# Two channels in a 32-row tile: a product-quantized convolution pair regrouped from 88 tiles of three channels to 128 tiles of two

## The chip, the cores and the metric

The kernel runs on one core of one Trainium2 chip. The metric is the device time of one execution in microseconds (us), the median of several executions. A ratio is the mean time of one kernel's runs over the mean time of the other kernel's runs of the same rounds, with a 95% interval; it is therefore not quite the ratio of the medians that stand beside it.

Names: TensorE is PE in the profile, VectorE is DVE, ScalarE is ACT, GpSimd is POOL, SyncE is SP.

Words: an engine *issues* a transfer, and the transfer *lands* when the last of its end records comes in. A *turn* is a transpose on VectorE. *Half clock* is a stretch in which the trace records a granted TensorE clock of 0.5, and one such stretch is a *spell*. The *maxima* are the largest logits of a softmax, taken out before the exponential.

## The reference

Sixteen images of 256 channels and 28x28 pixels go through group norm, then twice through a convolution in which every 3x3 patch of every channel is replaced by a softmax mixture of that channel's 16 centroids. Batch norm, a squeeze-and-excite gate and two residual additions follow.

```python
def amm_conv3x3(x, centroids, w_sub, stride=1):
    B = x.shape[0]
    C, k, s = centroids.shape                       # 256, 16, 9
    patches = jax.lax.conv_general_dilated_patches(x, (3, 3), (stride, stride), 'SAME')
    p = patches.reshape(B, C, s, Ho * Wo).transpose(0, 3, 1, 2)
    d = jnp.sum(p * p, axis=-1)[..., None] - 2.0 * jnp.einsum('bncs,cks->bnck', p, centroids) \
        + jnp.sum(centroids * centroids, axis=-1)[None, None]
    attn = jax.nn.softmax(-d, axis=-1)
    lut = jnp.einsum('cks,cso->cko', centroids, w_sub)
    return jnp.einsum('bnck,cko->bno', attn, lut)...
# per image: x + relu(se(bn2(amm(relu(bn1(amm(gn(x))))))) + gn(x))     [cut]
```

## The kernel before

An image's two layers are worked in halves of 384 and 400 pixels. The nine shifted copies of the image (the patches) are written to DRAM by ScalarE (`to_pat`) and loaded again as rows of tiles (`patches`). A tile of 32 rows holds three channels. The 88 tiles make 11 groups of eight, so two halves and two layers make 44 slots per image. A slot has one group of *logits* (eight products of 31x64), the exponential of it, one group of *numerators* (eight products of 64x32) of the slot before, and three or four *lookups* (full 128x128 products that add the result into two accumulators).

```python
def to_pat(l, i, pat):                               # patch writes, ScalarE's hardware queue
    dx, pieces = STEPS[i]
    for j, k, p0, n, rt in (PIECES[i] for i in pieces):
        ...
        nc.scalar.dma_start(view(pat, ...), ...)

def finish(b, k, i):                                 # last residual of an image, four times per image
    y, xt = ys[b][0][half(k, i)], xs[b][half(k, i)]
    rstd, _ = nrm[b]
    nc.vector.scalar_tensor_tensor(y, xt, rstd[:, k : k + 1], y, op0=ALU.mult, op1=ALU.add)
    nc.vector.scalar_tensor_tensor(y, y, 0.0, xt, op0=ALU.max, op1=ALU.add)

def patches(u):                                      # one load of 128 rows for two groups, GpSimd's software queue
    ...
    nc.gpsimd.dma_start(
        pt[:, : 2 * len(gs), :n],
        view(u["pat"], 2 * gs[0] * P * HW + px, [[HW, P], [P * HW, 2 * len(gs)], [1, n]]),
    )

def logits(u, gi, rows):
    l, g, n = u["l"], u["groups"][gi], u["px"][1]
    ps = [pair(), pair()]
    for i in range(4):
        for h in range(2):
            nc.tensor.matmul(
                ps[i // 2][64 * h : 64 * h + 64, i % 2, :n],
                lhsT=wd[l][32 * i : 32 * i + rows, 2 * g + h, :],
                rhs=u["pt"][32 * i : 32 * i + rows, 2 * gi + h, :n],
                start=True, stop=True,
            )
    return ps

# the order inside the program, slot s of a group (the second number is the place in the slot)   [cut]
at(s, 5, b_logits, u, gi)
at(s, 6, b_exp, u, gi)
at(s + 1, 3, b_num, u, gi)                           # numerators one slot after their exp
at(s + 1, 4, b_turn, u, gi)
at(s + 1, 4, c_scale, u, gi)
at(s + 2, 2, c_turn, u, gi)
at(n - self.lead - (self.lb if mx else 0), 9, patches, u)
```

Some tiles of the second layer also need their maxima first. Their logits are computed once ahead, reduced on VectorE, sent to DRAM and back on SyncE (`m_out`, `m_in`) into the tile `pm`.

## Time and profile before

| | before |
|---|---|
| median of 3 runs | 3248.12 us (3246.1 to 3253.05) |
| span of the profiled run | 3240.9 us, clock 0.980 |
| TensorE / VectorE / ScalarE / GpSimd busy | 95% / 76% / 46% / 41% |
| image period in the quiet part | 188.6 us |

TensorE is the bound; the lines that carry this are shown in the prediction below.

### The profile page before, as it was taken

Reading aid. Unit: us, or ns where it says so; the run is one execution under the profiler, and the core shown is the slowest. Engines: PE = TensorE matmul, PEld = TensorE weight load, DVE = VectorE, ACT = ScalarE, POOL = GpSimd, SP = SyncE. Lnnn points to the kernel's source line nnn. Section 1 sums busy time; section 2 is a strip of 40 time slices with the busy share of each in tenths; the row PEclk is TensorE's granted clock in tenths of the full one; section 3 lists DMA queues with packets and bytes.
Section 4 is the critical chain, followed back from the end, with each engine's and each line's share of the span. In section 5 each row is a group of like instructions: output and inputs, shape, how many; then the busy total and the mean of one; then the engine's idle time right before and its main releaser. Section 6 shows DMA issues by size and latency. Waiting matters only on the chain.

```text
span 3240.9 us, 72313 instructions
## 1 busy us (share of the span) xinstructions
PE 3079.0 (95%) x29086; PEld 1208.6 (37%) x29086; DVE 2479.0 (76%) x4133; ACT 1506.0 (46%) x2507; POOL 1330.1 (41%) x1427
## 2 busy tenths in 40 slices
PE   3489999999999999999999999999999999999997
PEld 2233333333333333333333333333333333334333
DVE  2156778788787878878787887878788787878786
ACT  1144455454545545454544545445454545545343
POOL 1033444444444444444443444444344444434342
PEclk7689999999999999999999999999999999999999
DMA  7465555575655557565555756555575555556532
GB/s 228 119 191 170 166 177 178 175 230 178 195 184 176 179 173 230 178 195 183 176 175 177 229 179 194 176 175 181 180 229 179 194 180 177 178 177 220 173 111 65
DMA packets 232373, 586.02 MB, mean 181 GB/s; under 512 B 76238, under 2 KB 89182, under 8 KB 232030
## 3 DMA queue, kind: packets, MB, share of 16 engines
q0 software_dynamic: 76544, 321.16, 31.9%
q10 hardware_dynamic: 82666, 238.70, 22.5%
q1 hardware_dynamic: 72820, 21.45, 3.3%
q8 instruction: 232, 3.80, 0.5%
q14 instruction: 111, 0.91, 0.1%
HBM read 328.23 MB, written 257.82 MB: 181 GB/s over the span
## 4 chain that ended last, share of the span: by engine, by line
PE 70%; DVE 17%; DMA 6%; POOL 3%; issue 2%; ACT 1%; SPq 0%; ACTq 0%; POOLq 0%; DVEq 0%
PE acc L722 38%; PE pair L571 17%; PE pair L645 13%; DVE nt L657 4%; DVE q L711 4%; POOL nt L684 3%; DVE rc L661 3%; DVE y L538 2%; DMA xt<-in_x 1%; DVE z L590 1%; DMA pat<-in_consts 1%; DVE gn_st L426 1%; DVE y L539 1%; DMA ws<-dws 1%; DMA dm<-mt 1%
## 5 line engine op out<-in xcount | busy, mean ns | idle before, releaser
L722 PE MATMUL acc<-q,ws 128*128 128x384 f32 (+1 forms) x4608 | 1732.9, 511 | 0.6 <-ACT y L745 0.6
L635 ACT ACTIVATE e<-pair 128x768 f32<-128x768 f32 (+1 forms) x1408 | 1084.6, 821 | 1351.2 <-PE pair L571 1268.0
L684 POOL TENSOR_TENSOR nt<-nt,rc 128x648 f32<-128x648 f32 (+1 forms) x576 | 773.2, 1342 | 1404.6 <-DVE rc L661 1180.3
L722 PEld LDWEIGHTS acc<-q,ws 128*128 128x128 f32 x4608 | 811.3, 190 | 911.0 <-issue 463.6
L711 DVE STREAM_TRANSPOSE q<-nt 128x768 f32<-128x768 f32 (+1 forms) x576 | 577.6, 1003 | 424.7 <-POOL nt L684 380.0
L657 DVE STREAM_TRANSPOSE nt<-pair 128x768 f32<-128x768 f32 (+1 forms) x704 | 692.3, 983 | 157.2 <-PE pair L645 153.9
L645 PE MATMUL pair<-e,cw 64*32 64x384 f32 (+1 forms) x11264 | 639.2, 505 | 60.6 <-ACT e L635 49.3
L571 PE MATMUL pair<-pt,wd 31*64 31x384 f32 (+1 forms) x9216 | 558.1, 517 | 9.1 <-DVE z L590 9.1
L661 DVE RECIPROCAL rc<-nt 128x72 f32<-128x72 f32 (+1 forms) x704 | 438.6, 623 | 24.2
L690 POOL TENSOR_TENSOR qx<-nt,rc 128x324 f32<-128x324 f32 (+3 forms) x256 | 179.0, 739 | 406.8 <-DVE rc L661 406.8
L645 PEld LDWEIGHTS pair<-e,cw 64*32 64x32 f32 x11264 | 131.0, 105 | 440.4 <-ACT e L635 207.0
L700 ACT COPY nt<-qx 128x120 f32<-128x120 f32 (+1 forms) x576 | 184.5, 320 | 238.0 <-DVE rc L661 228.7
L571 PEld LDWEIGHTS pair<-pt,wd 31*64 31x64 f32 x9216 | 143.3, 130 | 400.0 <-issue 340.2
L556 POOL DMA_DIRECT2D pt<-pat x288 | 228.6, 794 | 36.2 <-DMA pat<-side 35.9
L590 DVE STREAM_TRANSPOSE z<-pair 128x768 f32<-128x768 f32 (+1 forms) x192 | 182.7, 989 | 68.9 <-PE pair L571 68.9
L571 PE MATMUL pair<-pm,wd 31*64 31x384 f32 (+1 forms) x3584 | 224.9, 513 | 6.9 <-DVE nt L657 5.4
L596 DVE TENSOR_REDUCE mx<-z 128x48 f32<-128x768 f32 (+1 forms) x192 | 186.2, 970 | 0.0
L664 DVE TENSOR_REDUCE ext<-rc 128x1 f32<-128x72 f32 (+1 forms) x608 | 140.5, 231 | 20.8
L665 DVE TENSOR_REDUCE ext<-rc 128x1 f32<-128x72 f32 (+1 forms) x608 | 134.2, 221 | 0.0
L571 PEld LDWEIGHTS pair<-pm,wd 31*64 31x64 f32 x3584 | 61.0, 129 | 146.5 <-issue 52.8
L556 POOL DMA_DIRECT2D pm<-pat x128 | 94.9, 742 | 8.6 <-DMA pat<-side 8.6
L538 DVE SCALAR_TENSOR_TENSOR y<-xt,gn_rstd,y 128x392 f32<-128x392 f32 x64 | 76.9, 1202 | 0.8 <-ACT y L532 0.8
(106 smaller groups left out, 720.6 us busy)
## 6 DMA issues: line engine op xcount, KB each, us to landing
pt<-pat POOLq DMA_DIRECT2D x144, 800.0 KB, 7.5
pt<-pat POOLq DMA_DIRECT2D x144, 768.0 KB, 5.7
pat<-side ACTq DMA_DIRECT2D x128, 771.8 KB
pat<-im ACTq DMA_DIRECT2D x64, 771.8 KB
pat<-side ACTq DMA_DIRECT2D x64, 404.2 KB
pm<-pat POOLq DMA_DIRECT2D x64, 400.0 KB, 6.1
xt<-in_x POOLq DMA_DIRECT2D x32, 784.0 KB, 8.0
pm<-pat POOLq DMA_DIRECT2D x64, 384.0 KB, 4.1
```

Of the source, the lines that this page charges most:

```text
L556: nc.gpsimd.dma_start(pt[:, : 2 * len(gs), :n], view(u["pat"], 2 * gs[0] * P * HW + px, [[HW, P], [P * HW, 2 * len(gs)], [1, n]]),)
L571: nc.tensor.matmul(ps[i // 2][64 * h : 64 * h + 64, i % 2, :n], lhsT=wd[l][32 * i : 32 * i + rows, 2 * g + h, :], rhs=u["pt"][32 * i : 32 ...
L590: nc.vector.transpose(z[:, : 64 * nb].rearrange("p (i m) -> p i m", i=2), ps[:, :, : 32 * nb])
L596: nc.vector.tensor_reduce(u["mx"][:, a : a + 2].rearrange("p i (c b) -> p i b c", c=2)[:, :, :nb], u["z", gi].pop(0)[:, : 64 * nb].rearran ...
L635: nc.scalar.activation(e[:, :, :n], ps[:, :, :n], AF.Exp, scale=2.0)
L645: nc.tensor.matmul(ps[32 * i : 32 * i + 32, h, :n], lhsT=cw[l][64 * h : 64 * h + 64, g, i, :], rhs=es[i // 2][64 * h : 64 * h + 64, i % 2, ...
L657: nc.vector.transpose(t[:, : 2 * nb].rearrange("p (h b) r -> p h (b r)", h=2), u.pop(("nm", gi))[:, :, : 32 * nb])
L661: nc.vector.reciprocal(rc[:, : 2 * nb], t[:, : 2 * nb, SUM : SUM + 3])
L684: nc.gpsimd.tensor_tensor(v, v, rc[:, : 2 * nb].unsqueeze(3).to_broadcast([P, 2 * nb, 3, 9]), ALU.mult)
L700: nc.scalar.copy(u["nt", gi][0][:, : 2 * nb].rearrange("p (h b) r -> p h b r", h=2)[:, :, :, SUM:], bass.AP(w.tensor, w.offset, [list(w.ap ...
L711: nc.vector.transpose(q[:, : 64 * nb], t[:, : 2 * nb].rearrange("p b r -> p (b r)"))
L722: nc.tensor.matmul(accs[key][:, :n], lhsT=ws[l][:, 2 * g + h, o * P : (o + 1) * P], rhs=u["q", gi][:, 32 * nb * h : 32 * nb * h + n], star ...
```

## The change

Its intent is less work on TensorE: a tile of 32 rows holds two channels, so a group is 16 products of 32x32 that run side by side instead of eight larger ones. Eight groups of sixteen tiles make 32 slots per image instead of 44, at nearly the same cost per group. The rest follows from that layout: patch tensors of 18 dense rows (no constant fill), four loads of 18 rows per tile on SyncE, dense numerators, numerators in the slot of their exp with lookups split around them, the second step of the finish on ScalarE and GpSimd, and the watch on the sums on GpSimd. The sorting of weights moves from the start into the first slots. (Where loads are counted, "tile" means the patches of one such group: one load tile that holds sixteen of the 32-row tiles.)

```diff
-NCH = 3
-NRT = 88
+NCH = 2
+NRT = 128
+ROWS = 9 * NCH
...
-    d_pat = [dram.tile([NRT * 32, HW], F32, name=f"pat{i}") for i in range(3)]
+    d_pat = [dram.tile([NRT * ROWS, HW], F32, name=f"pat{i}") for i in range(3)]
...
-    def clear_pat(i): ...            # constants into the patch tensors
+    for t in pts + pms:              # constants once, into fixed tiles (4 pts, 2 pms)
+        nc.sync.dma_start(t[ONE::32], ...)
...
     def to_pat(l, i, pat):           # 12 writes per image and layer, still on ScalarE
-        for j, k, p0, n, rt in (PIECES[i] for i in pieces):
-            nc.scalar.dma_start(...)
+        nc.scalar.dma_start(
+            view(pat, (ROWS * p0 + 9 * k + 3 * dx) * HW, [[ROWS * HW, n], [HW, 3], [1, HW]]), ...)
...
     def finish(b, k, i):
         nc.vector.scalar_tensor_tensor(y, xt, rstd[:, k : k + 1], y, op0=ALU.mult, op1=ALU.add)
-        nc.vector.scalar_tensor_tensor(y, y, 0.0, xt, op0=ALU.max, op1=ALU.add)
+        nc.scalar.activation(y, y, AF.Relu)
+        nc.gpsimd.tensor_add(y, y, xt)
...
     def patches(u):
-        nc.gpsimd.dma_start(pt[:, : 2 * len(gs), :n], ...)
+        for i in range(4):
+            nc.sync.dma_start(
+                pt[32 * i : 32 * i + ROWS, :, :n],
+                view(u["pat"], (16 * u["m"] + i) * ROWS * HW + px, [[HW, ROWS], [4 * ROWS * HW, 4], [1, n]]),
+            )
...
-    def logits(u, gi, rows):
-        for i in range(4):
-            for h in range(2):       # 8 products
+    def logits(u, rows):
+        for t in range(4):
+            for i in range(4):       # 16 products
+                c = 32 * ctile(i, t)
                 nc.tensor.matmul(
-                    ps[i // 2][64 * h : 64 * h + 64, i % 2, :n], ...
+                    ps[t // 2][c : c + 32, t % 2, :n], ...
...
+    LOGITS, EXP, LOOK_A, NUM, TURN, SMALL, LOOK_B, MAX, LOOK_C, TURN_BACK, REST = range(11)
```

## The prediction

No term of its sum is among them: it still comes to 174.9 + 8.4 + 2.9 + 1.5 + 3.5 + 1 = 192 us per image, of which the author took 190.

> **What bounds the kernel now.** I read the page first (busy shares and slices), then the chain of work that ended last, then a table over one stretch of it, then the timeline of a few microseconds inside it.
>
> ```profile
> PE 3079.0 (95%) x29086; PEld 1208.6 (37%) x29086; DVE 2479.0 (76%) x4133; ACT 1506.0 (46%) x2507; POOL 1330.1 (41%) x1427
> ...
> PE   3489999999999999999999999999999999999997
> ```
>
> TensorE (PE) is busy 95%; only the first three slices (81 us each) are thin. The chain of waits shows the steady rhythm, because the same burst of four lookup products comes back once per image:
>
> ```profile
> 2256.30 2.88 PE acc L722 x8
> 2322.09 2.88 PE acc L722 x8
> 2334.47 2.88 PE acc L722 x8
> 2350.67 2.88 PE acc L722 x8
> 2444.94 2.88 PE acc L722 x8
> ```
>
> 2444.94 - 2256.30 = 188.6 us per image. The table over that stretch (busy us of PE, weight loads, DVE, ACT, POOL, then clock, DMA share, GB/s):
>
> ```profile
> 2256.30:2445.00 188.70, 187.61 (x1809) 72.88 (x1810) 154.16 (x255) 93.28 (x155) 82.55 (x88) 1.00 0.60 188
> ```
>
> PE 99.4%, clock 1.00: here PE sets the time. 16 x 188.6 = 3018 us; the other 3241 - 3018 = 223 us is the start (the first logits group runs at 116 us and slots limp until 170) and some 20 us of end. The timeline shows one slot (columns: start, duration, engine, line):
>
> ```profile
> 1603.26 0.88 PE L645 MATMUL pair<-e,cw 64*32 64x384 f32 x16
> ...
> 1604.07 0.90 PE L571 MATMUL pair<-pt,wd 31*64 31x384 f32 x16
> 1604.42 0.94 DVE L657 STREAM_TRANSPOSE nt<-pair 128x768 f32<-128x768 f32 x1
> ...
> 1604.90 2.28 PE L722 MATMUL acc<-q,ws 128*128 128x400 f32 x6
> 1605.07 1.51 ACT L635 ACTIVATE e<-pair 128x768 f32<-128x768 f32 x2 [2.14 <-PE pair L571]
> 1605.40 0.60 DVE L661 RECIPROCAL rc<-nt 128x72 f32<-128x72 f32 x1
> ...
> 1607.11 0.88 PE L645 MATMUL pair<-e,cw 64*32 64x384 f32 x16
> ```
>
> To see: numerators (8 small products, 16 instructions[...]) hold PE from 1603.26 to 1604.07, 0.81 us; logits 0.83; three lookups 2.21. For the 400-column half the same starts give 0.84, 0.85; lookup bursts give 2.13 (3) and 2.78 (4) at 384 columns, 2.21 and 2.88 at 400, so about 0.19 per burst plus 0.66 per product. Exp starts 1.00 after the logits, two take 1.51, and they hide behind three or four lookups: numerators of a group run one slot later.
>
> Check of this arithmetic on before: per image 44 slots x (0.82+0.84) = 73.0; 144 lookups x 0.66 = 95.0; 50 bursts x 0.19 = 9.5; 6 extra logits groups 5.0; six waits of 0.47 after them (groups of 1.31 instead of 0.83) 2.8; small products about 2. Sum 187.3, measured 188.6.
>
> [...] Here first rounds of the 8 tiles start 6.7 ns apart in the trace[...]. [...] the new layout has four row tiles writing one bank, in different quadrants. No run shows that case yet; it is a risk. [...]
>
> **The change part by part, per image.**
>
> Small products. Groups fall from 44 to 32 for logits and for numerators, extra logits from 6 to 4. A group has 16 products, so eight more starts: 0.05 us (8 x 6.7 ns), giving 0.86 + 0.88 (384) or 0.89 + 0.90 (400), mean 1.77 for the pair. 32 x 1.77 = 56.6 against 73.0: saves 16.4.
>
> Lookups. 16 tiles of dense numerators and 2 of tails: 36 products per half image and layer, as before. 95.0 us stays. But they now stand in two bursts per slot (two between logits and numerators, two or three behind): 64 + 4 bursts x 0.19 = 13.0 against 9.5: loses 3.5. Extra logits 3.5 against 5.0; small products 2.
>
> Exp in the same slot. Two lookups after the logits end at 0.88 + 1.48 = 2.36 us after their start; the second exp is done at 1.00 + 1.51 + 0.06 (release to start as seen at 218.98) = 2.57. The second half of the numerators waits about 0.15: x 32 = 4.8.
>
> Sum so far 56.6 + 95.0 + 13.0 + 3.5 + 2 + 4.8 = 174.9, a slot of 5.27 us. This is 13.7 us (7%) less than before. DVE per slot: two transposes 0.97, reciprocal of 96 to 104 (604 ns for 72, 642 for 78, so 0.75 to 0.8), transpose back 1.0: 3.65 of 5.27. POOL: scaling 768 to 832 elements (1293 ns for 648) 1.6, tails and two sums 1.1: 2.7, which has a slot to hide in. ACT exp 1.54. None becomes the bound on average. The two range reductions (141 + 134 us), the fills (185 us ACT) and the POOL load issues (324 us) go from engines with room: worth nothing directly.
>
> **What is given back: work that crosses engines at the slot's end.**
> - The finish. The second DVE step becomes an ACT Relu and a POOL add. DVE reaches the first step only after turns, reciprocal and transpose back, 3.65 us after the numerators end; each takes 1.2. The two Relus (0.7) thus end at 5.6 and 6.75, two gates follow (1.4), and only then ACT takes the next exp, due at 2.8. PE waits for it: about 5.2 us, then 3.2 in the next slot, which has no gates. 8.4 per image. Before had both steps on DVE.
> - Group norm. Statistics fall in slots with the maximum work: DVE ends 6.9 us after the numerators where PE wants them after 5.3: 1.7. Two later hops through POOL cost about 0.5 and 0.7. Together 2.9.
> - Maxima. Between the turn of the maxima and the logits that use them are now some 7.5 us (17 before). The round trip through DRAM took 4.5 us when quiet and 8 to 15 beside patch writes. About 1.5.
> - DMA. Second-layer patches (7.2 MB) are written two pieces per slot, 228 GB/s, beside loads of 0.45 MB per slot[...]. At the start before's writes alone got about 240 GB/s, and issues blocked ACT up to 2.4 us. Estimate 3 to 4.
>
> 174.9 + 8.4 + 2.9 + 1.5 + 3.5 + 1 for evacuations = 192; with halves of these gains and losses in doubt I take 190.
>
> Start. No constant fill of the patch tensors (ACT sat 20.6 us behind it, later 18.3 again), and weight sorting (46 to 116 us) moves among the slots. First slot near 56, about 45 us of sorting products remain, plus 30 to 35 of stalls: 136 lost instead of 203. With 20 of end, 156 against 223: saves 67.
>
> **Sum:** 16 x 190 = 3040, less 8 for the last image's finish, plus 156 = 3188. I put 3190.
>
> **Rivals.**
> 1. The packing gain comes through whole: the ACT block is shorter than worked out. For it: 7% is a large and well-measured term. Against: [...]the program order is plain. Then 16 x 179 + 156 = 3020 to 3050.
> 2. Tiles sharing a bank, or 64 instructions per group, slow the groups by 0.1 us or more. For: [...]no group here has more than 32 instructions with weight loads. Against: [...]starts are 6.7 ns apart. 68 groups x 0.1 x 16 = 109 us: about 3300[...].
> 3. Transfers become the wait[...]. For: DMA already shows shares near 0.8 in bursts. Against: bytes fall (18 rows of 32 used), and loads are issued some four slots ahead. If exp and loads wait through both layers' writes, 5 to 10 us per image more: 3270 to 3350.
> 4. DVE becomes the bound. Its 3.65 of 5.27 us speaks against it, except in slots with maxima.
>
> **Range and chances.** The image period may be off by 7 us either way (112 us in all) and the start by 25: 3060 to 3320. The 2% line is 3183, almost at my value; rival 1 pulls below it, 2 and 3 above. Faster 0.45, same 0.45, slower 0.10.
>
> **What would show it.** Right: groups of 32 PE instructions lasting 0.86 to 0.90 from start to next burst; slots near 5.3; numerators waiting for ACT e in every slot by 0.1 to 0.2 and, twice per image, by 3 to 5 us with a Relu just ahead of that exp; a first slot near 56 us. Wrong: groups above 1.0 us; no long waits for exp; POOL or SyncE loads named ahead of logits; a period under 180 or above 200.

## More of the kernel before

One more view matters later, so it is given here: the waits of TensorE before (engine, line, what it waited for; then us in total, times, longest), from 270 to 3150 us of the span.

```profile
PE pair L571 <- DVE z L590: 9.1, 13, 1.8
PE pair L645 <- ACT e L635: 7.3, 4, 3.9
```

These are the two largest; all that the view lists come to 28 us in 2880, and none is a DMA. There is nothing to win from waits; only less work on TensorE can help.

## The result

| | before | after |
|---|---|---|
| median | 3249.12 us (3246.1 to 3253.05, 4 runs) | 3380.34 us (3372.49 to 3393.12, 4 runs) |
| ratio after/before | | 1.0407 [1.0371, 1.0443] |
| clock of the profiled run | 0.980 | 0.950 |

The change made the kernel slower by 4%, outside the predicted range. The outputs are correct. From the page after, busy times, the granted clock in 40 slices, and the chain that ended last by engine:

```profile
PE 3042.2 (90%) x39838; PEld 1195.0 (35%) x39838; DVE 2250.0 (67%) x2756; ACT 1094.9 (32%) x1611; POOL 1501.8 (45%) x2165
...
PEclk9888999999999999999999999999999999999998
...
PE 62%; DMA 16%; DVE 12%; issue 4%; ACT 2%; POOL 2%; SPq 1%; ACTq 1%; DVEq 0%; POOLq 0%
```

TensorE is no longer busy throughout (90% for 95%), and DMA now has 16% of the chain (6% before). The same table over one image period as in the prediction (busy us of PE, weight loads, DVE, ACT, POOL, then clock, DMA share, GB/s):

```profile
2057.01:2261.20 204.19, 186.76 (x2482) 72.54 (x2481) 139.35 (x168) 67.51 (x99) 93.42 (x134) 0.95 0.61 159
```

This period has 17 us in which TensorE is idle and a clock of 0.95. Measured from the first small product of the squeeze-and-excite step of one image to that of another, eleven images apart, the period is 200.6 us on average (190.2 before, measured in the same way). Predicted were 190.

The timeline of a few microseconds shows what is right and what is wrong (start, duration, engine, line, operation, tiles, shape, count; in brackets the idle time just before and its releaser):

```profile
2047.57 0.93 PE L543 MATMUL pair<-pt,wd 19*32 19x384 f32 x32
...
2049.96 1.09 PE L611 MATMUL pair<-e,cw 32*32 32x384 f32 x32
2050.98 1.61 PE L675 MATMUL acc<-q,ws 128*128 128x400 f32 x4
...
2053.19 0.83 PE L543 MATMUL pair<-pt,wd 19*32 19x384 f32 x4
2054.98 2.03 PE L543 MATMUL pair<-pt,wd 19*32 19x384 f32 x28 [0.96 <-DMA pt<-pat]
2056.95 2.93 PE L675 MATMUL acc<-q,ws 128*128 128x384 f32 x4
```

The logits group at 2047.57 takes 0.86 us to the next start, as worked out. The one at 2053.19 stops after four of its 32 instructions, because the other loads of its tile have not landed: the next two lookups (four instructions) start at 2056.95 instead of some 2054.05. And those lookups then take 2.93 us instead of 1.56 (the two at 2050.98 took 1.61 with 400 columns). The granted clock in the records is 0.5 from 2056.4 on, for 3.4 us. So this late load is paid twice: by the wait, and by TensorE at half clock after it.

The waits of TensorE after, from 270 to 3150 us:

```profile
PE pair L611 <- ACT e L601: 72.5, 42, 3.6
PE pair L543 <- DMA pm<-dm: 67.2, 23, 4.5
PE pair L543 <- DMA pt<-pat: 49.7, 24, 3.9
PE pair L409 <- DVE gn_mv L404: 23.5, 14, 1.7
```

In 28 us of waits before there was no DMA; now there are 117 us for transfers: patches (`pt<-pat`) and maxima (`pm<-dm`). The view even counts too little: a group that stops in its middle, as above, is shown with less idle time than it lost (0.96 us for the 1.8 us from 2053.2 to 2054.98), because the model of overlapping products covers part of the gap. I added up the gaps between the starts of neighbouring products in the trace, where the instruction between them waits for a semaphore of a SyncE or ScalarE transfer: 58.2 us within the logits groups (34 times). Most of these stops are in the view's 49.7 us already: 43.5 of them lie within groups and only 6.3 before a group. So the loads cost 6.3 + 58.2 = 64.5 us of waiting.

Why do loads come late? The queue of SyncE itself says what each load stood waiting for before it was issued (same window):

```profile
SPq L530 <- DMA pat<-im: 352.0, 68, 12.3
SPq L530 <- DMA pt<-pat: 348.1, 469, 4.7
SPq L582 <- DVE mt L575: 322.0, 48, 17.6
SPq L530 <- PE pair L543: 302.9, 197, 8.4
SPq L530 <- DMA pat<-side: 249.9, 84, 6.9
```

`pat<-im` and `pat<-side` are the patch writes of ScalarE. In none of these waits does the load read what the write is writing: that is a later stage's tensor. The instruction list explains it. Every transfer counts its end on a semaphore, and this program has eight for all transfers of SyncE and ScalarE together (numbers 108 and 110 to 116 in the trace) and eight others for GpSimd's (100 to 107). They are used strictly in turn: the 2407 issues of SyncE and the 392 of ScalarE, each in its own order, merge into one rotation over the eight, 349 or 350 times round. And none of the 2799 was issued before the last landing record that the trace holds of the previous user of its semaphore. Before, SyncE issued about 490 transfers, ScalarE 512 and GpSimd 464 (416 of them patch loads). After, SyncE issues 2407 and ScalarE 392 over the same eight, and GpSimd only 48. So a load waits for whatever stood eight transfers before it, and often that is a 588 KB write that ScalarE issued late. In all 152 of the waits for `pat<-im` and `pat<-side` above, the semaphore waited for is the one that the load itself is about to use. The maxima's transfers on SyncE stand behind writes in the same way, for 78 us in this window. The chain around the timeline above shows one such case (start, duration, what):

```profile
2039.68 7.37 DMA pat<-im
...
2047.07 0.02 SPq L530
...
2047.48 8.35 DMA pt<-pat
...
2055.87 1.15 PE pair L543 x26
2057.01 2.86 PE acc L675 x4
```

A write issued at 2039.68 lands at 2047.05; only then does SyncE issue the load (L530), which lands at 2055.83, and TensorE goes on.

### The profile page after: what moved, and what is told of

Read it like the earlier page. It is cut to its first block, busy times and chain, and to the rows that moved or that the text cites. A ratio compares the mean times of both kernels' runs of the same rounds, so it can differ in the third digit from the quotient of the medians.

```text
span 3371.0 us, 94072 instructions
## 1 busy us (share of the span) xinstructions
PE 3042.2 (90%) x39838; PEld 1195.0 (35%) x39838; DVE 2250.0 (67%) x2756; ACT 1094.9 (32%) x1611; POOL 1501.8 (45%) x2165
## 4 chain that ended last, share of the span: by engine, by line
PE 62%; DMA 16%; DVE 12%; issue 4%; ACT 2%; POOL 2%; SPq 1%; ACTq 1%; DVEq 0%; POOLq 0%
PE acc L675 35%; PE pair L611 13%; PE pair L543 12%; DMA pt<-pat 6%; DVE nt L623 4%; DMA pm<-dm 3%; DMA dm<-mt 3%; DMA pat<-side 2%; DVE q L657 2%; DMA pat<-im 2%; DVE y L511 2%; DVE rc L629 1%; DVE mx L567 1%; ACT e L601 1%; POOL k L639 1%
## 5 line engine op out<-in xcount | busy, mean ns | idle before, releaser
L623 DVE STREAM_TRANSPOSE nt<-pair 128x832 f32<-128x832 f32 (+1 forms) x1024 | 978.3, 993 | 1042.8 <-PE pair L611 907.8
L639 POOL TENSOR_TENSOR k<-nt,rc 128x832 f32<-128x832 f32 (+1 forms) x512 | 803.5, 1569 | 1829.7 <-DVE rc L629 1827.4
L601 ACT ACTIVATE e<-pair 128x800 f32<-128x800 f32 (+1 forms) x1024 | 787.0, 820 | 1692.4 <-PE pair L543 1691.9
L611 PE MATMUL pair<-e,cw 32*32 32x384 f32 (+1 forms) x16384 | 624.0, 527 | 83.6 <-ACT e L601 83.6
L543 PE MATMUL pair<-pt,wd 19*32 19x384 f32 (+1 forms) x14336 | 479.0, 513 | 76.2 <-DMA pt<-pat 75.7
L657 DVE STREAM_TRANSPOSE q<-k 128x832 f32<-128x832 f32 (+1 forms) x512 | 488.9, 955 | 0.8 <-POOL k L639 0.8
L629 DVE RECIPROCAL rc<-nt 128x104 f32<-128x104 f32 (+1 forms) x512 | 398.4, 778 | 17.6
L645 POOL TENSOR_TENSOR tail<-nt,rc 128x104 f32<-128x104 f32 (+1 forms) x512 | 236.0, 461 | 0.0
L675 PE MATMUL acc<-qt,ws 128*128 128x400 f32 (+1 forms) x512 | 220.9, 514 | 0.0
L651 POOL TENSOR_TENSOR total<-total,nt 128x96 f32<-128x96 f32 (+1 forms) x448 | 208.9, 466 | 0.0
```

The lines of the kernel that those rows point to most:

```text
L543: nc.tensor.matmul(ps[t // 2][c : c + 32, t % 2, :n], lhsT=wd[l][32 * i : 32 * i + rows, 4 * u["m"] + t, :], rhs=u["pt"][32 * i : 32 * i + ...
L601: nc.scalar.activation(e[:, :, :n], ps[:, :, :n], AF.Exp, scale=2.0)
L611: nc.tensor.matmul(u["nm"][t // 2][32 * i : 32 * i + 32, t % 2, :n], lhsT=cw[l][c : c + 32, 4 * u["m"] + t, :], rhs=es[t // 2][c : c + 32, ...
L623: nc.vector.transpose(nt[:, :nb, 2 * v : 2 * v + 2].rearrange("p b t r -> p t b r"), ps[:, :, : 32 * nb].rearrange("p t (b r) -> p t b r", ...
L629: nc.vector.reciprocal(rc[:, : 8 * nb], u["nt"][:, :, SUM])
L639: nc.gpsimd.tensor_tensor(q[:, :nb].rearrange("p b (a s) -> p (b a) s", s=8), nt[:, :, :8], rc.unsqueeze(2).to_broadcast([P, 8 * nb, 8]), ...
```

## The experiments

Twelve kernels were run. Theory A: the loads are late because they share the order of eight semaphores with the patch writes, and long waits cost half clock besides. The bandwidth rival: the transfers themselves are the limit (many more loads: 2048 for 416 before). The finish rival: the loss is the finish and its crossings between engines.

### noload: no patch loads at all

```diff
         loads[mx] += 1
+        u["pt"] = pt
+        if u["b"] != "g":
+            if loads[mx] > len(tiles):
+                return               # every later tile uses old data: wrong on purpose
+            px, n = 0, 400
```

> Wrong result on purpose: each patch buffer is loaded once and then reused; patch writes, maxima trips and all arithmetic stay. If the loss comes from loads that land late[...], the 54 us of TensorE waits on pt<-pat and the half-clock time behind them go, and the maxima trip no longer queues behind loads: 3100 to 3220 us. If the loss lies in the arithmetic itself (16 products per group, exp in the same slot) or in the finish alone, it stays above 3300 us.

Measured: 3211.67 us (3199 to 3214), ratio 0.987 [0.9835, 0.9906]; the result is wrong, as meant. The time is inside the first range. The waits for `pt` are gone, and loads are worth 5.4 points of ratio (1.0407 less 0.987), some 170 us. What is left is 40 us for the maxima, 76 for ScalarE's exp and 24 for the group norm (270 to 3000 us).

### wpool: patch writes from GpSimd

```diff
-        nc.scalar.dma_start(
+        nc.gpsimd.dma_start(
             view(pat, (ROWS * p0 + 9 * k + 3 * dx) * HW, ...
```

> The patch writes are issued from GpSimd instead of ScalarE; same bytes[...], same slots. Theory A ([...]loads stand behind 5 to 8 us writes): SyncE no longer waits for pat<-im and pat<-side (608 us of its queue in the kernel after), TensorE waits on pt<-pat and pm<-dm (125 us) at least halve, 3220 to 3300 us. Theory B (bandwidth: loads[...] beside write bursts land late however they are issued): within 1% of 3380 us, TensorE waits as before.

Measured: 3194.29 us (3192 to 3198), ratio 0.9828 [0.9798, 0.9857], correct. The bytes are the same, and so are the loads and their queue. One word is changed, and 186 us are gone. SyncE's waits now, from 270 to 3000 us:

```profile
SPq L582 <- DVE mt L575: 612.8, 58, 17.7
SPq L530 <- PE pair L543: 576.9, 289, 8.8
SPq L530 <- DMA pt<-pat: 140.9, 288, 2.5
...
SPq L530 <- DMA pat<-side: 66.5, 15, 6.6
```

And the two largest waits of TensorE in the same window (after the change 67.2 and 63.8 us there, with 47.3 for `pt<-pat` besides):

```profile
PE pair L611 <- ACT e L601: 73.7, 42, 3.4
PE pair L543 <- DMA pm<-dm: 27.5, 11, 4.5
```

The 602 us of waits for writes in front of loads (352.0 + 249.9; 572 of them in this shorter window) have become 66.5 (for `pat<-side`, 15 times), and these 15 are for writes that the waiting load does read, about one per image. TensorE waits for no patch load any more, before a group or within one; its waits for the maxima have more than halved. The longest waits are now for a buffer to come free or for the maxima, which means that SyncE runs ahead. In the trace I paired every load with its last landing record. A load took 5.1 us from issue to landing in the kernel after (median of 1500; nine in ten under 7.0), and 5.8 here (nine in ten under 8.0). So the loads themselves became *slower*, and the time still fell. What changed is when they are issued: the last of a tile's four loads was issued 12.0 us before its logits in the kernel after (median; one in twenty under 5.3), and 16.4 here (one in twenty under 7.8). This refutes the bandwidth rival as the main cause and fits theory A; the time lies below its recorded range. That ScalarE was relieved of issuing does not explain the gain: TensorE's waits for its exp did not fall (73.7 us).

### findve: the finish's second step back on VectorE

```diff
-        nc.scalar.activation(y, y, AF.Relu)
-        nc.gpsimd.tensor_add(y, y, xt)
+        nc.vector.scalar_tensor_tensor(y, y, 0.0, xt, op0=ALU.max, op1=ALU.add)
```

> The second step of the finish goes back to VectorE in one instruction (no ScalarE Relu, no GpSimd add). Theory of the prediction: TensorE waits on ACT e (77 us, 44 of them) fall below 30 us and with the half-clock time behind them 80 to 110 us go: 3270 to 3305 us. If DMA waits swallow the gain (the loads are late anyway), under 40 us go: above 3340 us.

Measured: 3305.6 us (3304.5 to 3309.3), ratio 1.0174 [1.0144, 1.0205]: 75 us less than after, just outside the range of its first reading. TensorE's waits for exp (`ACT e`) fall from 72.5 to 11.1 us (270 to 3150 us):

```profile
PE pair L610 <- ACT e L600: 11.1, 18, 1.4
```

The finish rival is real, but it is the smaller part; the waits for loads and maxima stay (42 and 86 us, against 50 and 67 after the change).

### pairload: one load for two tiles

```diff
-    pts = [const.tile([P, 4, 400], F32, name=f"pt{i}") for i in range(4)]
+    pts = [const.tile([P, 8, 400], F32, name=f"pt{i}") for i in range(3)]
...
-                pt[32 * i : 32 * i + ROWS, :, :n],
+                pt[32 * i : 32 * i + ROWS, : 4 * len(us), :n],   # us: this tile and the next
...
# room for it: epool 4 -> 3 buffers, kpool 3 -> 2
```

> One patch DMA brings two tiles (8 column blocks of 18 rows) wherever two neighbouring tiles need no maxima, three double buffers in place of four single ones; bytes[...] and lead stay. Theory A (issue held by semaphores of earlier DMAs): 2304 loads become 1280, SyncE waits on pt<-pat (365 us) about halve, TensorE waits on pt<-pat mostly go, 3260 to 3330 us. Theory B (bandwidth[...]): same bytes[...], within 1% of 3380 us.

Measured: 3354.78 us (3351 to 3360), ratio 1.032 [1.0288, 1.0351]. The number was missed: 1280 loads in place of 2048 (the 2304 of the expectation is a miscount) gained only 25 us. SyncE's waits say why:

```profile
SPq L535 <- DMA pat<-side: 299.5, 90, 12.2
SPq L535 <- DMA pat<-im: 248.6, 57, 9.1
```

548 us in front of loads, for 602 in the kernel after. Fewer loads share the eight with the same writes, so each stood behind one more often: 147 such waits from 270 to 3150 us with 1280 loads in the run, 152 with 2048 in the kernel after. And a paired load took 8.6 us to land (median) instead of 5.1. Fewer loads did not help while the writes stayed among them. What the smaller `epool` and `kpool` cost was not separated.

### both, both_max, both_look3: the repairs together, and two refinements

`both` is wpool and findve in one kernel. `both_max` adds the maxima's last reduction, turn and sending one slot earlier, `both_look3` a third lookup ahead of the numerators:

```diff
-                        at(a + 2, TURN_BACK, a_max, u, 1)
-                        at(a + 2, TURN_BACK, m_turn, u)
-                        at(a + 2, TURN_BACK, m_out, u)
+                        at(a + 1, TURN_BACK, a_max, u, 1)        # both_max
+                        at(a + 1, TURN_BACK, m_turn, u)
+                        at(a + 1, TURN_BACK, m_out, u)
...
-                        self.at(s, LOOK_A if i < 2 else ...
+                        self.at(s, LOOK_A if i < 3 else ...      # both_look3
```

> Patch writes on GpSimd and the finish on VectorE together. If the two losses are separate (186 us and 75 us measured one at a time against 3380), they add: 3105 to 3135 us, TensorE waits on ACT e below 15 us and no waits on pt<-pat. If they overlap (the same gaps in TensorE), it stays at 3150 to 3190 us.

> The same, and both maximum reductions, the turn of the maxima and their write to memory come one slot (about 5.3 us) earlier; the slots of use stay. Theory: the 37 us of TensorE waits on pm<-dm and the half-clock time after each come from a round trip that is a few us too long for its slot budget; both go, 30 to 60 us less than the run without it: 3060 to 3095 us. Rival: the trip waits for DMA capacity, so an earlier start changes under 10 us; or VectorE, with 1 us more in that slot, makes TensorE wait for it instead (waits on z or nt above 20 us).

> Writes on GpSimd and finish on VectorE, with three lookups instead of two between the logits and the numerators of a slot. The prediction's own term: the second half of the numerators waits some 0.15 us for the second exp in each of 512 slots (77 us). If that is so the numerator groups shrink from 1.03-1.10 to 0.86-0.90 us and 50 to 80 us go against the run without it: 3040 to 3080 us. If the last lookups are then too short to hide the turn of the numerators, waits on DVE nt appear instead and it gains under 20 us.

Measured:

| | median us | ratio to before | image period us |
|---|---|---|---|
| both | 3093.69 (3068.55 to 3099.53) | 0.9494 [0.9443, 0.9545] | 183.8 |
| both_max | 3195.46 (3195.08 to 3201.07) | 0.9839 [0.9809, 0.9869] | 191.0 |
| both_look3 | 3168.64 (3162.89 to 3173.45) | 0.9745 [0.9714, 0.9775] | 188.9 |

`both` is faster than the kernel before by 5%, a little under the range of 3105 to 3135 us. It gives 9.1 points of ratio over the kernel after, where the single repairs give 5.8 and 2.3: a little more than their sum (by 1.0, where the intervals allow some 0.8 of noise). It also has fewer spells of half clock. The clock records from 270 to 3000 us have 242 us of half clock after the change (51 spells), 133 in wpool (27), 229 in findve (42) and 58 in `both` (12); before had 10 (2). But noload, with no wait for patch loads at all, still had 218 (36), so the half clock does not come from the loads alone. One of its quiet image periods in the table over a stretch:

```profile
1323.00:1504.00 181.00, 177.58 (x2504) 70.35 (x2480) 142.24 (x172) 66.08 (x97) 105.54 (x155) 1.00 0.66 179
```

181.0 us at full clock. This is the period that the packing makes possible.

`both_max` takes away the waits that it was built to take away, those for the maxima, and still loses 102 us, a size that no reading named. The longest of SyncE's waits in `both` (270 to 3000 us):

```profile
SPq L581 <- DVE mt L574: 626.6, 62, 16.8
```

The same line in `both_max`:

```profile
SPq L581 <- DVE mt L574: 831.4, 59, 19.3
```

And one stop of TensorE in the timeline of `both_max`:

```profile
2082.75 4.20 PE L542 MATMUL pair<-pt,wd 19*32 19x400 f32 x32 [0.26 <-DMA pt<-pat]
2086.88 3.04 PE L674 MATMUL acc<-q,ws 128*128 128x400 f32 x4
```

SyncE stands in front of the maxima's sending (L581) for 831 us instead of 627, because VectorE has not turned them yet, and the patch loads stand behind it in SyncE's order. In one tile of twenty the last load was issued 1.7 us or less before its logits (7.4 in `both`). Each of the four loads then lets a few products through, so the group takes 4.20 us instead of 0.95 with only 0.26 of idle time in the view, and the lookups after it run at half speed (3.04). This is the same fault as in the kernel after, with VectorE in the place of the writes.

`both_look3` loses 75 us. Its first reading missed; its second (waits for VectorE's `nt`, which grew from 7.0 to 18.5 us) named the direction and not the size. The loads are as early as in `both` (one in twenty under 7.1 us). The prediction's own term is real: the numerator groups shrink from 1.13 to 0.95 us on average, which is worth some 90 us in 512 of them. But its logits groups take 1.21 us on average, 0.96 in `both`, and so give back some 110 us in the 448 of them that need no maxima; the bursts of lookups grow too (1.47 to 1.52 us). Gaps in the logits groups behind VectorE's semaphore have grown from 21 to 47 us; the waits that the counting ties to a semaphore do not make up the whole 75 us. That VectorE's turn of the numerators no longer hides behind only one or two lookups is the likely reason, but it was argued, not shown.

### before_sync: the kernel before with its loads on SyncE

```diff
-        nc.gpsimd.dma_start(
+        nc.sync.dma_start(
             pt[:, : 2 * len(gs), :n],
```

> The kernel before with its patch loads issued from SyncE instead of GpSimd, one DMA of 128 rows per two groups as it has them. If it is the hardware queues as such (shared by loads and patch writes) that delay loads, TensorE waits on pt<-pat appear and it takes 3280 us or more. If it is the number of DMAs (four per tile, eight completion semaphores turning over in two tiles), this kernel has one load per two groups, eight DMAs back is some five slots back, and it stays within 1% of 3250 us.

Measured: 3276.67 us (3272.6 to 3278.6), ratio 1.0079 [1.0049, 1.0109]. This is inside the 1% of the second reading. With one load of 128 rows for two groups, issued further ahead, the move costs 0.8%. SyncE still waits 259 us for writes in front of these loads, but never for the semaphore that the load itself is about to use. So the move to SyncE alone is not the loss; it appears to take the many loads beside the writes as well.

### both_gn, both_mg, both_gnmg: what is left in `both`

```diff
-            self.at(t + 2, SMALL, gn_mean, b)
-            self.at(t + 3, SMALL, gn_var, b)
-            self.at(t + 4, REST, gn_apply, b, 0)      # and 1
+            self.at(t + 3, SMALL, gn_mean, b)          # both_gn: each one slot later
+            self.at(t + 4, SMALL, gn_var, b)
+            self.at(t + 5, REST, gn_apply, b, 0)      # and 1
...
-            nc.sync.dma_start(view(d, 32 * p0, ...      # both_mg: m_out and m_in from GpSimd
+            nc.gpsimd.dma_start(view(d, 32 * p0, ...
```

> The version with both repairs (patch writes from GpSimd, the second step of the finish on VectorE; 3094 us), with the group norm's two small products and what follows each one slot later. Theory: in the version with both repairs TensorE waits 23.6 us in all for VectorE before the first of these products (14 times, 1.7 each) and 6.9 us for GpSimd before the second[...]. If a slot more hides them: no such wait left, 20 to 35 us less, 3055 to 3080. Rival: VectorE runs late at that place anyway (a burst of normalization work), so the wait moves to the next group: within 10 us of 3094.

> The version with both repairs, with the maxima's four small transfers of a tile issued by GpSimd rather than SyncE. What is left of TensorE's waits for transfers in the version with both repairs is for the maxima coming in (38 us in 15 waits, longest 8.6), and SyncE stands 627 us in front of the maxima going out, ahead of patch loads. Theory: SyncE's order is what makes these late, so freed of it the wait falls under 20 us and the time to 3060 to 3085. Rival: GpSimd's own order is as bad (it runs the scaling of the denominators, and the patch writes stand in its queue too): the wait stays or grows, or VectorE waits for GpSimd's totals: 3095 to 3160.

> Both of the edits of this call together. If each gives what its theory says, they add up: 3030 to 3060. If the maxima's transfers are no gain from GpSimd, this is within 15 us of that kernel less what the later products gave.

Measured: both_gn 3095.38 us (3093.32 to 3112.7), ratio 0.9539 [0.9508, 0.9571]: no gain, within 2 us of `both`, as its rival said. TensorE's waits name the trade. Two lines of `both` (270 to 3000 us):

```profile
PE pair L409 <- DVE gn_mv L404: 23.6, 14, 1.7
PE pair L610 <- ACT e L600: 8.1, 14, 0.6
```

In both_gn the first of them is not there any more, and the second reads:

```profile
PE pair L610 <- ACT e L600: 30.4, 28, 1.6
```

The 23.6 us for VectorE's statistics are gone, and waits for exp have grown by 22 us: the wait moved to the next group, as the rival expected, though at ScalarE and not at VectorE.

both_mg: 3178.1 us (3168.36 to 3184.85), ratio 0.9785 [0.9763, 0.9807], a miss, and beyond the rival's range too, but in the rival's way. The loads are now issued 20.5 us ahead (median), but the maxima come in later: 58.7 us of waits for `pm<-dm` in place of 38.4, and 29.4 for a group norm step on GpSimd in place of 6.9. GpSimd waits 128 us in front of the maxima's return, with everything else that it does behind. both_gnmg: 3148.12 us (3139.81 to 3150.69), ratio 0.9678 [0.9658, 0.9698]; also a miss. Beside both_mg it is 30 us faster, so there the later group norm does pay; beside both_gn it is 53 slower.

### pairload_pool: the loads leave instead of the writes

```diff
-            nc.sync.dma_start(
+            nc.gpsimd.dma_start(
                 pt[32 * i : 32 * i + ROWS, : 4 * len(us), :n],
```

> The version with one load per two tiles (3355 us), its patch loads issued from GpSimd instead of SyncE; the patch writes stay on ScalarE. Moving the writes to GpSimd (3194 us) may have helped because loads and writes no longer share one set of eight completion semaphores, or because writes themselves behave better in GpSimd's kind of queue. Here the writes stay where they were and the loads leave. Theory A (shared set): no load waits for a write it does not need (now 548 us of waits in front of loads), TensorE's waits for pt under 10 us (35 now), time 3190 to 3290, the more as issuing costs GpSimd some 0.6 us a load. Rival (the writes' own queue): loads still come late, pt over 25 us, time over 3330. Third: GpSimd's order is too full (it scales in front of lookups): TensorE waits for VectorE's q or nt behind GpSimd, whatever the loads do; then the waits for pt alone decide between the first two.

Measured: 3813.34 us (3802.43 to 3828.41), ratio 1.1739 [1.17, 1.1778]. It answers another question than the one it was made for. By the rule the rival won: waits for `pt` are 90.7 us. But the records show that no load stood behind a write, and that a paired load took 8.1 us to land (8.6 from SyncE). What changed is that GpSimd issues loads (0.62 us each, median) behind the scaling of the same slot, so that 53% of them were issued less than 8 us before their logits (18% in pairload). The largest wait of TensorE is for the maxima, 150.2 us (45 in pairload): their transfers stayed on SyncE beside the writes, and once per image their sending stood behind a write (14 waits). The clock records have 514 us of half clock from 270 to 3150 us. The run agrees with late issue being what costs, and leaves the test inconclusive on the sharing itself.

## Why the prediction was wrong

**Right: the packing.** The step "32 x 1.77 = 56.6 against 73.0: saves 16.4" holds: logits groups take 0.86 (384 columns) and 0.89 (400) to the next start, numerators 1.03 to 1.10 with the expected wait of 0.15 to 0.2 for the second exp. The sum of 174.9 plus 2.9 for the group norm and 1 for evacuations is 178.8; the quiet period of `both` is 181.0. So the gain per image was there, 7.6 us below the quiet period before. Two small slips in the working change nothing: a slot of 5.27 us leaves out the extra logits and the small products (174.9 over 32 slots is 5.47), and VectorE's 3.65 us are 3.7 by their own parts. Rival 2, tiles that slow each other, did not happen: with four row tiles that write different quadrants of the same columns of `pair` the outputs are correct, neighbouring starts lie 7 ns apart (median) and groups take the 0.86 us above. What the 0.19 us per burst is was not shown; no run tested it.

**Right: the start.** First slot at 46.8 us, predicted near 56. The span less sixteen periods of 200.6 is 161 us, predicted 156.

**Right in kind, too large: the finish.** "PE waits for it: about 5.2 us, then 3.2 in the next slot" was 8.4 per image. The waits for exp measure 72.5 us in 14.4 images, 5.0 each, and taking the finish back was worth 75 us, 4.7 per image. The group norm's waits of 1.7 came exactly so.

**The step that failed: "DMA. ... Estimate 3 to 4", and with it "Maxima. ... About 1.5".** Together they priced the waits for transfers at some 5 us per image. Measured per image: 4.5 for loads (64.5 us in 14.4 images) and 4.7 for the maxima (67.2), with half clock besides. Moving the writes alone gave back 186 us, or 11.6 per image. So the size of the load term was near; its mechanism, and with it the maxima and the half clock, were not. The text reasoned on bytes per second (and on a number of engines). Bytes per second are not the limit: wpool kept the bytes and the loads, and removed the waits for loads and more than half of those for the maxima. What was left out is that a load is issued in an order that it shares with slow writes on another engine. The code could have warned: no view of the profile before shows the sharing, but the loads went out on GpSimd, whose queue the page calls software_dynamic, and the change moved them to SyncE's, hardware_dynamic like the one that already carried ScalarE's writes. The rival that came nearest said "If exp and loads wait through both layers' writes, 5 to 10 us per image more: 3270 to 3350". Its size was near, which was luck in part, for its stated cause, a number of engines for the loads, was shown by no run.

**The term that was missing: half clock.** The prediction has no line for it. Before the change 3 spells of half clock cover 14 us from 270 to 3150 us; after it 54 spells cover 256 us. Each has a gap of 1 us or more between the starts of neighbouring products in the 9 us before it. At half speed 256 us cost at most 128 us, or 8.9 per image. That is more than all waits for loads and maxima beyond the prediction (1.0 + 3.2 per image). The trace agrees on the half: two lookups take 2.93 us at the granted clock of 0.5 and 1.56 otherwise. Short waits are among those with a spell, too: six of the fourteen waits of 1.7 us for the group norm have one that begins within 2 us of their end.

Put together per image, against the 192 that the prediction's terms summed to: loads +1.0, maxima +3.2, half clock at most +8.9, finish -3.4, group norm about -0.9. That is 192 + 8.8 = 200.8; measured were 200.6. That it closes so well is luck in part, because not all of the 8.9 need be lost and the working's own check on the kernel before was off by 1.3.

**Open.** That loads wait for the semaphores of writes is read from the records, and that moving the writes removes these waits is shown. Whether another property of GpSimd's kind of queue (software_dynamic on the page) helps as well was not separated, since pairload_pool brought its own delay. What sets off the half clock was not tested by itself. Why `both` and both_gn have periods from 180.5 to 189 us within one execution stays open too.

## What to carry to other kernels

Before moving transfers to another engine, list what else counts on the same completion semaphores, in program order, and ask for each load what stands before it on its own semaphore (in this program, eight issues back). In the kernel after, loads that land in 5.1 us (median) stood up to 12.3 us behind a write that they do not read. Price a long wait of TensorE with the half clock that follows it. In the kernel after, 43 of the 50 idle gaps of 2 us or more had a spell begin in them or in the 7 us behind them, 8 of the 21 from 1.6 to 2 us, and 4 of the 37 from 0.5 to 1.6. And look inside groups: a group with 0.26 us of idle time in the view had taken 4.20 us instead of 0.95 (`both_max`), and of the 58.2 us lost within logits groups after the change the view shows 43.5. The best version found here keeps the packing, issues the patch writes from GpSimd and the finish on VectorE: 3094 us, 5% below the kernel before.
